# Layer 1's one-head attention and gate written between the chunks of layer 0's last two shared blocks, and layer 3's gate computed with its columns held in TensorE

## The chip, the core and the metric

The kernel runs on one core of a Trainium2 chip. The time is the device time of one execution in microseconds (us), the median of several runs; beside it stands one profiled execution with its span, from the first instruction to the last. The engines named are TensorE (PE, with its weight loads PEld), VectorE (DVE), ScalarE (ACT), GpSimd (POOL) and SyncE (SP), which issues most of the DMAs. Each engine works through its own instructions in the order in which they stand in its queue.

## The reference

A stack of four layers works on x, 2 sequences of 1,024 tokens of 256 values. Each layer adds a gated cross-attention to 77 context keys and then a gated feed-forward part, each on a normalised copy of x:

```python
x = x + tanh(g_xattn[l]) * xattn_l(layernorm(x), ctx, ctx, ...)
x = x + tanh(g_ffn[l])   * ffn_l(layernorm(x), ...)
```

Layers 0, 2 and 3 have 16 attention heads. Layer 1 has one head of width 256:

```python
Q = q @ Wq.T + bq;  K = k @ Wk.T + bk;  V = v @ Wv.T + bv
softmax(Q @ K.T / 16) @ V
```

The feed-forward parts are mixtures of experts, except layer 2's, which is quantised. Layer 0 has 8 experts, of which each token takes two, and a shared expert that every token takes; each is `swiglu((x@w1+b1)*(x@w3+b3))@w2+b2`. Layer 1 sends each token to the best of 16 experts; an expert takes at most 128 tokens, in the order of the tokens, so the places can be counted only when every token has its choice:

```python
gate = softmax(x @ Wg);  idx = argmax(gate)
loc = sum((cumsum(one_hot(idx)) - 1) * one_hot(idx))
```

Layer 3 takes `sigmoid(x @ gate_w)` over 8 experts in 4 groups, keeps two groups and two experts in them, and adds a shared expert too.

## The kernel before

**Tiles.** x lies on chip as 16 tiles `xs[i]` of 128 tokens by 256 values. Four of them make a block j of 512 tokens (`NB` = 4). A normalisation of a block (`layernorm`, L283-307) takes each tile's mean and variance on DVE (L290, L291), adds the small constant (L293), raises it to the power -1/2 on POOL (L295), makes four normalised tiles `h` on DVE (L299), turns them with eight transposes on TensorE into two PSUM banks `hTp` (L305), and copies these out, one on DVE (L306) and one on ACT (L307), as `hT`: channels on partitions, tokens along the row.

**Buffers.** PSUM has four banks for single results (`mm`) and two pairs of banks (`mm2`). The `h` tiles have four buffers in all, and the tiles `ga` into which expert outputs are gathered use the same four. Large weights (2 MB) have three buffers `wbig`; the attention's weights have one, `aw`.

**Order.** The code is written in an order of work, and a scheduler places its instructions in the engines' queues after that, with the waits that the data and the buffers need. Steps that are to overlap are therefore written between one another by hand: attention and expert jobs are generators that yield after each chunk.

**Layer 0's feed-forward part** (`ffn0`, L837-1052). After the gate, jobs run one after another (L1022-1041): shared blocks 0 and 1, 24 routed tiles of sorted tokens, shared blocks 2 and 3. A job's first half is `hidden` (L908-937): four chunks, each of two steps for a shared block; a step is four matmuls of 512 columns into one PSUM pair (L920), an eviction on ACT (L925) and one on DVE (L926). Its second half, `rest`, multiplies by the second weight (16 matmuls, L986) and adds to x (L990); it is written after the first chunk of the next job. When the last job is written, 32 gathers follow: for each tile two indirect DMAs from POOL (L1047), each added to x on DVE (L1051). Only then is a tile of x complete.

**Layer 1's attention** (`whole_attention`, L636-715) comes next: keys (L360) and values (L375) from the context once, then for each block the norm, the queries (L384 on TensorE, L663 on ACT), the scores (L671), the largest of them and the difference on DVE (L677, L679), the exponential on ACT (L680), the sums on DVE (L682-684), the probabilities turned on TensorE and copied on ACT (L690, L692), and the output (L700), weighted and added to x on DVE (L701). A loop staggers these steps over the blocks:

```python
for j in range(-2, NB + 1):
    has(turned, j)
    has(norm, j + 2)
    has(outputs, j)
    has(queries, j + 2)
    has(after, j - 1)
    has(scores, j + 1) if j >= 0 else None
```

`after` is `gate1` (L1060-1081): the norm for layer 1's experts, whose `h` tiles SP also stores to HBM, 32 small matmuls for the block's logits (`gate_logits`, L347), and the choice of the best expert on DVE, with an exponential on ACT. When all four blocks have their choice, `ffn1` counts the places: its first matmul is `cnt` (L1101). The experts' weights, 2 MB each, come by SP into the three `wbig` buffers.

**Layer 3's gate.** `turned(j)` (L1436) turns the normalised tiles of a block and copies them out (L1443, L1444). `gate` then computes the logits with `gate_logits`: for each of 16 tiles two matmuls with the turned tokens held in TensorE and 8 gate columns streamed. One sigmoid on ACT (L1453) reads the bank, and the choice of groups and experts on DVE follows, then the sorting, then the gathers of the routed tiles. The shared blocks' matmuls (`gus`, L1504) fill TensorE in the meantime.

Of the kernel before, what the change touches and what calls it, by code (L numbers as in the profile page):

```python
# [8 lines left out]
F32 = mybir.dt.float32  # L9
BF16 = mybir.dt.bfloat16  # L10
I32 = mybir.dt.int32
# [39 lines left out]
def flamingo_kernel(  # L51
# [18 lines left out]
    def mm(name, dt=F32, cols=512):  # L70
        return psA.tile([P, cols], dt, tag="mm", name=name)
# [237 lines left out]
    def new_hT(j, tagp):  # L309
        return hpool.tile([P, 2, TB], F32, tag=f"hT{j}", name=f"hT_{tagp}_{j}")  # L310
# [56 lines left out]
    def column(name, ec):  # L367
        c = COL[name]
        return cols[:, c, ec : ec + 1]
# [263 lines left out]
                behind(NB - 1)  # L633
        yield

    def whole_attention(l, after):  # L636

        w = attn_w.pop(l)
        scale = 1.0 / 16.0
        with ExitStack() as st:  # L640
            ap1 = st.enter_context(tc.tile_pool(name=f"at1_{l}", bufs=1))
            ap3 = st.enter_context(tc.tile_pool(name=f"at3_{l}", bufs=3))
            kT = ap1.tile([P, 2, 2 * NK], F32, tag="kT", name=f"kT{l}")
            pk = keys(l, "k", w, "k")
            for ec in range(2):
                V.tensor_scalar(kT[:, ec, :], pk[ec][:, 0 : 2 * NK], column(f"k{l}", ec), None, ALU.add)
            vs = []
            for b in range(2):
                vb = ap1.tile([NK, D], F32, tag=f"v{b}", name=f"vs{l}_{b}")
                pv = value(l, w, b)  # L650
                V.tensor_tensor(vb, pv[:NK, 0:D], w["bv"][:NK], ALU.add)
                vs.append(vb)
            hTs, qTs, prs, dens = {}, {}, {}, {}

            def norm(j):
                hTs[j] = new_hT(j, f"a{l}")
                layernorm(j, f"a{l}", hTs[j])

            def queries(j):
                qTs[j] = ap3.tile([P, 2, TB], F32, tag="qT", name=f"qT{l}_{j}")  # L660
                for ec in range(2):
                    pq = project(w, "q", hTs[j], ec, f"q{l}_{j}_{ec}")
                    S.activation(qTs[j][:, ec, :], pq, AF.Identity, bias=column(f"q{l}", ec))  # L663

            def scores(j):

                b = j // 2
                ps = mm(f"sc{l}_{j}")
                for k in range(4):
                    for ec in range(2):  # L670
                        T.matmul(  # L671
                            ps[:, k * NK : (k + 1) * NK], lhsT=qTs[j][:, ec, k * P : (k + 1) * P],
                            rhs=kT[:, ec, b * NK : (b + 1) * NK], start=(ec == 0), stop=(ec == 1),
                        )
                sc = ps[:, 0 : 4 * NK].rearrange("p (k n) -> p k n", n=NK)
                mx = ap3.tile([P, 4], F32, tag="mx", name=f"mx{l}_{j}")
                V.tensor_reduce(mx, sc, AX.X, ALU.max)  # L677
                pr = ap3.tile([P, 4, NK], F32, tag="pr", name=f"pr{l}_{j}")
                V.tensor_tensor(pr, sc, bcl(mx, NK), ALU.subtract)  # L679
                S.activation(pr, pr, AF.Exp, scale=scale)  # L680
                den = ap3.tile([P, 4], F32, tag="den", name=f"den{l}_{j}")
                V.tensor_reduce(den, pr, AX.X, ALU.add)  # L682
                V.reciprocal(den, den)
                V.tensor_scalar(den, den, tg[:, l : l + 1], None, ALU.mult)
                prs[j], dens[j] = pr, den

            def turned(j):
                pp = mm(f"pp{l}_{j}")
                for k in range(4):
                    T.transpose(pp[:NK, k * P : (k + 1) * P], prs[j][:, k, :], ident)  # L690
                prs[j] = ap3.tile([NK, TB], F32, tag="pT", name=f"pT{l}_{j}")
                S.copy(prs[j], pp[:NK, :])  # L692

            def outputs(j):
                for k in range(4):
                    i = 4 * j + k
                    if k % 2 == 0:
                        po = mm(f"o{l}_{i}")
                    half = po[:, (k % 2) * D : (k % 2 + 1) * D]
                    T.matmul(half, lhsT=prs[j][:, k * P : (k + 1) * P], rhs=vs[j // 2], start=True, stop=True)  # L700
                    V.scalar_tensor_tensor(xs[i], half, dens[j][:, k : k + 1], xs[i], ALU.mult, ALU.add)  # L701

            def has(step, j):
                if 0 <= j < NB:
                    step(j)

            for j in range(-2, NB + 1):
                has(turned, j)
                has(norm, j + 2)
                has(outputs, j)  # L710
                has(queries, j + 2)
                has(after, j - 1)
                has(scores, j + 1) if j >= 0 else None
                if j == -1:
                    scores(0)


    def route(nm, pool, pool2, oh, nf, nh, per, low, high):
# [107 lines left out]
        return sorted(range(nf + nh), key=lambda t: ((t + 0.5) / nf, 0) if t < nf else ((t - nf + 0.5) / nh, 1))  # L826


    wsh = {}

    def shared_first(n):
# [2 lines left out]
            out=wsh[n], in_=wbig0[8 * P * 4096 : 9 * P * 4096].rearrange("(r f) -> r f", f=4096)  # L834
        )

    def ffn0():  # L837
        h_dram = dram.tile([NT, D], F32, tag="h0_dram", name="h0_dram")
        eo_dram = dram.tile([NQ0 * P, D], F32, tag="eo0_dram", name="eo0_dram")
        with ExitStack() as st:  # L840
# [178 lines left out]
            wrow2 = f1.tile([P, nt], I32, tag="wrow2", name="wrow2")  # L1019
            V.tensor_scalar(wrow2, wrow, rest0, None, ALU.add)  # L1020

            jobs = [(shared, 0), (shared, 1)] + [(routed, t) for t in order] + [(shared, 2), (shared, 3)]  # L1022
            left = None
            for n, (job, arg) in enumerate(jobs):
                if n == 0:
                    load(order[0])
                    load(order[1])
                steps, rest = job(arg)
                for ic, _ in enumerate(steps):
                    if ic == 0 and left is not None:  # L1030
                        left()
                    if ic == 1 and n + 1 < len(jobs) and jobs[n + 1][0] is routed:
                        turn(jobs[n + 1][1])
                left = rest
                if job is routed:
                    at = order.index(arg) + 2
                    if at < nt:
                        load(order[at])
                    elif at == nt:
                        shared_first(1)  # L1040
                        shared_rest(1)
            left()
            prefetch(1)
            for i in range(NTI):
                for k in range(2):
                    ga = lnp.tile([P, D], F32, tag="h", name=f"ga0_{i}_{k}", bufs=4)
                    G.indirect_dma_start(  # L1047
                        out=ga, out_offset=None, in_=eo_dram,
                        in_offset=bass.IndirectOffsetOnAxis(ap=row[:, k * NTI + i : k * NTI + i + 1], axis=0),
                    )  # L1050
                    V.scalar_tensor_tensor(xs[i], ga, wk[:, k, i : i + 1], xs[i], ALU.mult, ALU.add)  # L1051


    NE, C, NF = 16, 128, 8
    h1_dram = dram.tile([NT, D], F32, tag="h_dram", name="h_dram")
    eo1_dram = dram.tile([NE * C, D], F32, tag="eo_dram", name="eo_dram")
    oh1 = gs1.tile([P, NTI, NE], BF16, tag="oh1", name="oh1")
    place1 = gs1.tile([P, NTI, 2, NE], BF16, tag="place1", name="place1")
    wgt1 = gs1.tile([P, NTI], F32, tag="wgt1", name="wgt1")
    row1 = gs1.tile([P, NTI], I32, tag="row1", name="row1")  # L1060

    def gate1(j):
        def keep(i, h):
            nc.sync.dma_start(out=h1_dram[i * P : (i + 1) * P, :], in_=h)

        hT = new_hT(j, "f1")
        layernorm(j, "f1", hT, each=keep)
        pl = gate_logits(j, hT, 8, NE, "f1")
        lg = gp.tile([P, NB, NE], F32, tag="g1l", name=f"g1l_{j}")
        V.tensor_copy(lg, pl)  # L1070
        blk = slice(4 * j, 4 * j + 4)
        first_max(lg, NE, oh1[:, blk, :], f"f1_{j}")

        V.tensor_scalar(place1[:, blk, 0, :], oh1[:, blk, :], iota_p, None, ALU.mult)
        V.tensor_tensor(place1[:, blk, 1, :], oh1[:, blk, :], bcl(tile128[:, blk], NE), ALU.mult)
        m = gp.tile([P, NB], F32, tag="g1m", name=f"g1m_{j}")
        V.tensor_reduce(m, lg, AX.X, ALU.max)
        V.tensor_tensor(lg, lg, bcl(m, NE), ALU.subtract)
        S.activation(lg, lg, AF.Exp)
        V.tensor_reduce(m, lg, AX.X, ALU.add)  # L1080
        V.reciprocal(wgt1[:, blk], m)

    def combine1(j):
        for i in range(4 * j, 4 * j + 4):
# [338 lines left out]
    def ffn3():  # L1423
# [4 lines left out]
        with ExitStack() as st:  # L1428
# [6 lines left out]
            def turned(j):  # L1435
# [7 lines left out]
                V.tensor_copy(hT[:, 0, :], pts[0])  # L1443
                S.copy(hT[:, 1, :], pts[1])  # L1444
                hTs[j] = hT

            def gate():

                pl = mm("lg_f3")
                for j in range(NB):  # L1450
                    gate_logits(j, hTs[j], 24, 8, "f3", pl[:, 32 * j : 32 * j + 32])
                sf = f1.tile([P, NTI, 8], F32, tag="g3s", name="g3s")
                S.activation(sf, pl[:, 0 : NTI * 8].rearrange("p (k n) -> p k n", n=8), AF.Sigmoid)  # L1453
                V.tensor_tensor(sf, sf, bcm(bc[:, 8:16], NTI), ALU.add)
                gs = f1.tile([P, NTI, 4], F32, tag="g3g", name="g3g")
                V.tensor_tensor(gs, sf[:, :, 0::2], sf[:, :, 1::2], ALU.add)
# [119 lines left out]

                return rest

            for j in range(NB):
                turned(j)  # L1580
            picked = gate()
# [49 lines left out]

    whole(heads_attention(0, ahead=lambda j: tables() if j == 2 else shared_first(0) if j == 3 else None))
    attn_w[1] = load_attn(1)
    ffn0()
    q2["pool"] = tc.alloc_tile_pool(name="w2p", bufs=1, side="right")
    whole_attention(1, gate1)
    attn_w[2] = load_attn(2)
    attn2 = heads_attention(2, combine1, norm2)
    next(attn2)
# [143 lines left out]
```

## Time and profile before

| | |
|---|---|
| time, median of 3 runs | 1594.83 us (1592.28 to 1599.27) |
| profiled execution: own time | 1592.78 us |
| its span | 1591.0 us |
| mean granted TensorE clock | 0.918 |
| instructions | 18,196 |
| TensorE busy in the 71.8 us from 654.4 (layer 0's last blocks) | 65.12 us, clock 0.98 |
| TensorE busy in the 88.9 us from 726.2 (layer 1's attention and gate) | 66.64 us, clock 0.72 |
| TensorE busy in the 52.5 us from 1383.0 (layer 3's gate and routing) | 43.56 us, clock 0.83 |

All times are of one profiled execution, in us from the start of the span. A row of the chain or of the waits begins with the start and the length of an instruction or group, then its engine, its line in the code and what it wrote and read; a bracket gives the time that the engine had stood idle before it and what ended that. A row of stage windows gives the window, its length, and the busy time of each engine with the number of instructions; the last three numbers are the granted clock (1 is full), the busy share of the DMA engines and what they moved in GB/s. Busy time is not the same as time on the path: what sets the end of a stage is read from the chain.

### The profile page before, as it was taken

The numbers are of one execution on the slowest core, as the hardware profiler recorded it, in microseconds if no ns is written. First come the engines' busy times: TensorE is split into PE (matmuls) and PEld (weight loads), VectorE is DVE, ScalarE is ACT, GpSimd is POOL, SyncE is SP. The second block draws the span as 40 slices with busy tenths as digits, with TensorE's granted clock in tenths as the row PEclk, the third lists the DMA queues.
The fourth block names the chain that finished last, engine by engine and source line by source line (L and its number), as shares of the span: only waits on it lengthen the run. The fifth ranks groups of instructions, "written<-read, shape, count | busy, mean of one in ns | idle before, by whom it ended". The sixth has DMA issues, their size and how long they took to land.

```text
span 1591.0 us, 18196 instructions
## 1 busy us (share of the span) xinstructions
PE 1370.0 (86%) x6844; PEld 914.4 (57%) x6844; DVE 888.3 (56%) x2167; ACT 399.5 (25%) x671; POOL 316.8 (20%) x367
## 2 busy tenths in 40 slices
PE   6999996999999999988759996899965999985773
PEld 3453444888888888445658883345334544544562
DVE  7676676444444444566543117667789666682124
ACT  1332430233333333212101111122354233201230
POOL 3200002212212120341021104300014300005651
PEclk9999997999999999999759997989987999987887
DMA  4001005555646555312216772000000000023535
GB/s 159 4 14 49 27 1 208 177 209 183 229 173 227 203 176 215 103 50 73 76 39 241 294 284 63 28 2 1 1 27 20 1 14 14 27 80 102 172 127 175
DMA packets 48363, 169.87 MB, mean 107 GB/s; under 512 B 9040, under 2 KB 27635, under 8 KB 42259
## 3 DMA queue, kind: packets, MB, share of 16 engines
q0 software_dynamic: 15600, 88.23, 15.9%
q1 hardware_dynamic: 25664, 74.33, 13.4%
q10 hardware_dynamic: 7010, 6.15, 1.3%
q8 instruction: 54, 0.88, 0.2%
q14 instruction: 35, 0.28, 0.1%
HBM read 147.97 MB, written 20.71 MB: 106 GB/s over the span
## 4 chain that ended last, share of the span: by engine, by line
PE 66%; DVE 16%; DMA 8%; issue 5%; POOL 2%; ACT 2%; another core or an unknown queue 1%; ACTq 0%; POOLq 0%; DVEq 0%; SPq 0%
PE hr L920 17%; PE hs L920 6%; PE sc L498 5%; PE eo L1004 4%; DMA wbig<-in_wbig_dram 4%; PE q L384 3%; PE as L574 3%; PE sT L546 3%; PE gur L1504 2%; PE h L1158 2%; PE av L574 2%; PE sT L553 2%; PE lg_f L347 2%; PE o L589 2%; PE eo_s L986 1%
## 5 line engine op out<-in xcount | busy, mean ns | idle before, releaser
L920 PE MATMUL hr<-xgT0s,w 128*128 128x256 f32 (+1 forms) x1536 | 299.9, 346 | 9.4 <-DVE ulr L926 9.2
L920 PEld LDWEIGHTS hr<-xgT0s,w 128*128 128x128 f32 x1536 | 246.3, 191 | 52.7 <-DVE ulr L926 22.1
L561 ACT ACTIVATE pT<-sT 78x1024 f32<-78x1024 f32 x96 | 92.7, 1015 | 231.8 <-PE sT L553 209.0
L498 PE MATMUL sc<-kbd,qT 128*128 128x308 f32 x384 | 126.6, 442 | 6.9 <-DVE qT L480 6.2
L920 PE MATMUL hs<-hT_f,w0s 128*128 128x512 f32 x256 | 119.4, 611 | 6.7 <-DVE x L1051 2.6
L508 DVE TENSOR_REDUCE nm<-sc 128x4 f32<-128x308 f32 x192 | 88.6, 474 | 46.3 <-PE sc L504 33.5
L926 DVE SCALAR_TENSOR_TENSOR ulr<-hr,w,ulr 128x256 f32<-128x256 f32 (+1 forms) x96 | 41.6, 433 | 127.0 <-ACT ulr L925 126.6
L579 DVE RECIPROCAL rz<-as 128x512 f32<-128x512 f32 x24 | 80.5, 3356 | 29.6 <-PE as L574 29.6
L498 PEld LDWEIGHTS sc<-kbd,qT 128*128 128x128 f32 x384 | 68.5, 197 | 44.4 <-issue 20.1
L920 PEld LDWEIGHTS hs<-hT_f,w0s 128*128 128x128 f32 x256 | 47.6, 195 | 59.8 <-issue 46.7
L925 ACT ACTIVATE ulr<-hr,w 128x256 f32<-128x256 f32 (+1 forms) x96 | 41.7, 434 | 143.6 <-PE hr L920 142.9
L1004 PE MATMUL eo<-w,hid_r 128*128 128x256 f32 x312 | 77.5, 379 | 0.0
L384 PE MATMUL q<-hT_a,aw 128*128 128x512 f32 x128 | 69.7, 678 | 6.5 <-DVE hT_a L306 4.5
L1158 PE MATMUL h<-xgTs,wbig 128*128 128x128 f32 x512 | 61.8, 281 | 6.6 <-DMA wbig<-in_wbig_dram 6.5
L948 POOL DMA_INDIRECT w<-in_wbig_dram,r_wr_f x24 | 24.2, 1008 | 212.9 <-PE hr L920 130.8
L1158 PEld LDWEIGHTS h<-xgTs,wbig 128*128 128x128 f32 x512 | 60.5, 196 | 9.9 <-issue 8.3
L1496 DVE TENSOR_TENSOR sg_r<-gur,sg_r 128x256 f32<-128x256 f32 (+1 forms) x24 | 9.0, 375 | 97.4 <-ACT sg_r L1495 64.0
L1004 PEld LDWEIGHTS eo<-w,hid_r 128*128 128x128 f32 x312 | 57.8, 190 | 7.6 <-issue 0.5
L1504 PE MATMUL gur<-xT3s,w 128*128 128x256 f32 (+1 forms) x192 | 50.6, 418 | 12.5 <-ACT xT3s L1552 9.1
L925 ACT ACTIVATE ugr<-hr,w 128x256 f32<-128x256 f32 (+1 forms) x96 | 41.7, 434 | 77.7 <-PE hr L920 70.9
L1171 PE MATMUL eo<-wbig,hh 128*128 128x256 f32 x256 | 59.9, 379 | 0.0
L926 DVE SCALAR_TENSOR_TENSOR ugr<-hr,w,ugr 128x256 f32<-128x256 f32 (+1 forms) x96 | 41.5, 432 | 31.4 <-ACT ugr L925 18.0
(451 smaller groups left out, 2305.9 us busy)
## 6 DMA issues: line engine op xcount, KB each, us to landing
wbig<-in_wbig_dram SPq DMA_DIRECT2D x17, 2048.0 KB
w<-in_wbig_dram SPq DMA_DIRECT2D x24, 384.0 KB
w0s<-in_wbig_dram SPq DMA_DIRECT2D x2, 2048.0 KB
h_dram<-h_f SPq DMA_DIRECT2D x32, 128.0 KB
y<-y_dram SPq DMA_DIRECT2D x4, 1024.0 KB
eo_dram<-eo0s SPq DMA_DIRECT2D x15, 256.0 KB
x<-in_x_dram SPq DMA_DIRECT2D x4, 512.0 KB
aw<-in_aw_dram SPq DMA_DIRECT2D x2, 1024.0 KB
```

The costliest lines, as they stand in the source:

```text
L384: T.matmul(pq, lhsT=w[m][:, dc, ec * P : (ec + 1) * P], rhs=hT[:, dc, :], start=(dc == 0), stop=(dc == 1),)
L498: T.matmul(ps[:, 0 : 4 * NK], lhsT=qTs[j][:, ec, k * P : (k + 1) * P], rhs=kbd[b][:, ec, 4 * hf : 4 * hf + 4, :].rearrange("p h k -> p (h ...
L508: V.tensor_reduce(nms[j][:, k, 2 * hf : 2 * hf + 2, ec, :], ps[:, 0 : 4 * NK].rearrange("p (r i k) -> p r i k", i=2, k=NK), AX.X, ALU.max, ...
L561: S.activation(pT[:, 2 * a : 2 * a + 2, :], pp[a][:NK1], AF.Exp, scale=scale)
L574: T.matmul(po[32 * r : 32 * r + 32, :], lhsT=lhsT(r, i)[:nk], rhs=pTs[j, ec, i][:nk, r, :], start=(i == 0), stop=(i == 1),)
L579: V.reciprocal(rz, pz)
L920: T.matmul(both[a][:, wi, :], lhsT=w13[:, dc, wi, a, ic * P : (ic + 1) * P], rhs=rhs(dc), start=(dc == 0), stop=(dc == 1),)
L925: S.activation(uu, both[a][:, 0, :], AF.Identity, bias=bias[:, 0, a, ic : ic + 1])
L926: V.scalar_tensor_tensor(uu, both[a][:, 1, :], bias[:, 1, a, ic : ic + 1], uu, ALU.add, ALU.mult)
L1004: T.matmul(po[:, s * D : (s + 1) * D], lhsT=hid[:, ic, s * P : (s + 1) * P], rhs=w2[:, ic, :], start=(ic == 0), stop=(ic == 3),)
L1158: T.matmul(ph[:, fc // 4, (fc % 4) * C : (fc % 4 + 1) * C], lhsT=w1[:, dc, fc * P : (fc + 1) * P], rhs=xgTs[e][:, dc, :], start=(dc == 0), ...
L1504: T.matmul(pa[:, s, 0:n], lhsT=w[:, s, dc, :], rhs=rhs(dc), start=(dc == 0), stop=(dc == 1))
```

## The change

**Layer 1 moves into layer 0.** `whole_attention` no longer runs its own loop. It makes the keys and values and gives back its five steps, which `ffn0` calls between the chunks of shared blocks 2 and 3. The gathers move as well: those of blocks 0 and 1 stand after the first chunk of shared block 2, with the keys and values, those of blocks 2 and 3 after its second and third chunk. `gate1` is split into `gate1_norm` (the norm with the stores) and `gate1` (logits and choice). What is left of attention and gate when shared block 3 is done is written behind it in a fixed order. The attention's pools lie on the other side of the on-chip memory, open from before `ffn0` to its end, with two buffers instead of three for `pr` and `pT`. The instructions of these steps themselves stay as they were.

**Layer 3's gate.** The 32 gate columns are now the held operand (8 of them are layer 3's, columns 24 to 31) and the turned tokens are streamed, 512 at a time: two matmuls for each block, written in `turned(j)` right behind its copies, into 32 partitions of one bank that is taken ahead of the first block. The result has tokens along the row, so two half copies (DVE and ACT) take it out, four transposes turn it back, and the sigmoid reads columns 24 to 31 of each group of 32.

```diff
-    def whole_attention(l, after):
+    def whole_attention(l, st):
...
+        return norm, queries, scores, turned, outputs
...
+    def gate1_norm(j):
+        def keep(i, h):
+            nc.sync.dma_start(out=h1_dram[i * P : (i + 1) * P, :], in_=h)
+
+        hT1[j] = new_hT(j, "f1")
+        layernorm(j, "f1", hT1[j], each=keep)
+
+    def gate1(j):
+        pl = gate_logits(j, hT1[j], 8, NE, "f1")
...
-            jobs = [(shared, 0), (shared, 1)] + [(routed, t) for t in order] + [(shared, 2), (shared, 3)]
+            jobs = [(shared, 0), (shared, 1)] + [(routed, t) for t in order]
...
+            s2, rest2 = shared(2)
+            next(s2)
             left()
             prefetch(1)
...
+            gathered(0)
+            gathered(1)
+            norm, queries, scores, turned1, outputs = whole_attention(1, st1)
+            next(s2)
+            gathered(2)
+            next(s2)
+            norm(0)
+            gathered(3)
+            next(s2)
+            queries(0)
+            norm(1)
+            s3, rest3 = shared(3)
+            next(s3)
+            rest2()
+            scores(0)
+            queries(1)
+            next(s3)
+            turned1(0)
+            scores(1)
+            norm(2)
+            next(s3)
+            outputs(0)
+            queries(2)
+            turned1(1)
+            next(s3)
+            gate1_norm(0)
+            scores(2)
+            outputs(1)
+            rest3()
+        gate1(0)
+        norm(3)
+        turned1(2)
+        gate1_norm(1)
+        queries(3)
+        outputs(2)
+        gate1(1)
+        scores(3)
+        gate1_norm(2)
+        turned1(3)
+        gate1(2)
+        outputs(3)
+        gate1_norm(3)
+        gate1(3)
...
+                for dc in range(2):
+                    T.matmul(
+                        pl[32 * j : 32 * j + 32, :], lhsT=gw[:, dc, :], rhs=hT[:, dc, :],
+                        start=(dc == 0), stop=(dc == 1),
+                    )
...
-                pl = mm("lg_f3")
-                for j in range(NB):
-                    gate_logits(j, hTs[j], 24, 8, "f3", pl[:, 32 * j : 32 * j + 32])
+                lgs = f3.tile([P, TB], F32, tag="sg", name="lgs3", bufs=4)
+                V.tensor_copy(lgs[:, 0:256], pl[:, 0:256])
+                S.copy(lgs[:, 256:512], pl[:, 256:512])
+                pt = mm("lgT_f3")
+                for k in range(4):
+                    T.transpose(pt[:, k * P : (k + 1) * P], lgs[:, k * P : (k + 1) * P], ident)
                 sf = f1.tile([P, NTI, 8], F32, tag="g3s", name="g3s")
-                S.activation(sf, pl[:, 0 : NTI * 8].rearrange("p (k n) -> p k n", n=8), AF.Sigmoid)
+                S.activation(
+                    sf.rearrange("p (j k) n -> p j k n", k=4),
+                    pt.rearrange("p (k j n) -> p j k n", k=4, j=4)[:, :, :, 24:32], AF.Sigmoid,
+                )
...
+            pl = mm("lg_f3")
             for j in range(NB):
                 turned(j)
...
-    ffn0()
+    with ExitStack() as st1:
+        ffn0(st1)
     q2["pool"] = tc.alloc_tile_pool(name="w2p", bufs=1, side="right")
-    whole_attention(1, gate1)
```

The queues that the moved steps pass: POOL has the 32 gathers, the powers of the norms and the memsets of layer 2's attention; SP has the stores of layer 1's `h` tiles, the expert weights and layer 2's attention weights.

## The prediction

> **What bounds the kernel now.** I read the page first: engines' shares, then the chain that ended last.
>
> ```profile
> PE 1370.0 (86%) x6844; PEld 914.4 (57%) x6844; DVE 888.3 (56%) x2167; ACT 399.5 (25%) x671; POOL 316.8 (20%) x367
> ...
> PE 66%; DVE 16%; DMA 8%; issue 5%; POOL 2%; ACT 2%; another core or an unknown queue 1%; ACTq 0%; POOLq 0%; DVEq 0%; SPq 0%
> ```
>
> TensorE carries two thirds of the chain, but that is a mean over stages. So I cut out the two stretches that the change merges: from the second chunk of shared block 2 to the end of shared block 3 (654.4 to 726.2), and one-head attention with layer 1's gate, up to the routing's first matmul, `cnt` (726.2 to 815.1). Columns: length, busy time of PE, its weight loads, DVE, ACT, POOL, then granted clock, DMA share, GB/s.
>
> ```profile
> 654.40:726.20 71.80, 65.12 (x179) 33.74 (x178) 46.41 (x106) 14.43 (x22) 32.01 (x33) 0.98 0.27 84
> 726.20:815.10 88.90, 66.64 (x288) 49.81 (x286) 49.01 (x176) 16.66 (x29) 9.32 (x12) 0.72 0.17 52
> 772.00:828.00 56.00, 33.58 (x143) 27.92 (x142) 29.14 (x111) 4.80 (x11) 7.94 (x11) 0.51 0.13 42
> ```
>
> The second stretch is bound by latency: no engine is full, and TensorE runs at 0.51 of its clock from 772 on. The chain within both, in order of time (start, length, what):
>
> ```profile
> 680.08 4.72 PE hs L920 x8
> ...
> 698.66 20.60 PE hs L920 x48
> 719.26 3.47 PE eo_s L986 x16
> ...
> 735.04 5.47 PE q L384 x8
> ...
> 742.32 3.67 PE q L384 x8
> ...
> 782.48 3.60 PE lg_f L347 x16
> ...
> 809.90 3.61 PE lg_f L347 x16
> ...
> 815.11 0.40 PE cnt L1101
> ```
>
> 48 records of `hs` in 20.6 us: a step (four matmuls, one PSUM pair) takes 3.43 us when fed. `q` takes 5.47 us after idleness and 3.67 us warm. Gathers are timed by POOL, and their adds sit between evictions in DVE's queue:
>
> ```profile
> 658.12 0.95 POOL L1047 DMA_INDIRECT ga<-eo_dram,r_row_f  x1 [52.99 <-DMA eo_dram<-eo0s]
> ...
> 660.83 0.48 DVE L1051 SCALAR_TENSOR_TENSOR x<-ga,wk,x 128x256 f32<-128x256 f32 x1 [0.86 <-DMA ga<-eo_dram,r_row_f]
> ...
> 680.08 3.70 PE L920 MATMUL hs<-hT_f,w0s 128*128 128x512 f32 x8 [1.62 <-DVE x L1051]
> ```
>
> TensorE idled there because the eviction that frees its PSUM pair stood behind a gather's add. Layer 3's gate, by the same chain:
>
> ```profile
> 1383.24 6.36 PE lg_f L347 x48
> 1389.60 1.91 PE gus L1504 x2
> 1391.51 3.21 PE lg_f L347 x16
> 1394.72 15.23 PE gus L1504 x32
> ```
>
> 64 small records take 9.6 us, at half clock by the end; DVE waits 11 us for them, then works 34.85 of 37 us (1398 to 1435) until the expert gathers start.
>
> **The change, part 1: up to the end of shared block 3.** The built kernel's order shows attention's work between the chunks as written. I walk it from 654.4 with rows of this trace. Keys and values now come first: `k` 1.21, `v` 1.89, together 2.95, so the next step starts at 657.4. Six steps remain, 20.6 us if fed. DVE's order puts 3 gather adds ahead of this chunk's first eviction, 7 ahead of the second, 15 ahead of the fourth. 20 gathers were issued from 658.12 to 682.36, 1.276 each, with the add 2.7 later: the 16th add can run at 658.12 + 15 x 1.276 + 2.7 = 680.0. With the eviction (0.75) the last step runs 680.9 to 684.3, 6.3 late.
>
> Block 0's norm waits for its power on POOL, queued behind the 24th gather: 658.12 + 23 x 1.276 + 1.25 = 688.7, power 1.05, h at 689.9. Behind it stand on TensorE the transposes, q and all of shared block 3: idle 684.3 to 690.4. q starts at 693.0. Taken cold, 5.47, it ends at 698.4, two steps of block 3 at 705.4. The last eight gathers take slots that h's transposes free at 691.0 (they share four); last issue 699.9, add 702.6, stats and an eviction, power, h: transposes 707.4 to 708.8. From there TensorE is fed, warm: block 2's output 7.07, sc 1.91, q 3.67, two steps 6.86, pp 0.66, sc 1.91, hTp 1.04, two steps 6.86, o 2.1, q 3.67, pp 0.66, two steps 6.86, hTp 1.04, sc 1.91, o 2.1, block 3's output 7.07: 55.4. With 1 us for short waits, E = 765.2. The merged work is 98 us of matmuls plus 8 us of the two idle stretches and 1.8 cold, where 72 us stood.
>
> **Part 2: from E to `cnt`.** Block 3 of x is complete only at E; its norm, query, scores, softmax, output, norm and gate remain, with other blocks' steps in the queues ahead. DVE: block 0's logits (1.93) and their copy stand ahead of the last stats: variance E+4.0, h E+5.4 (power with its waits 1.4). Transposes and copies, half clock, 3.0 (as 806.89 to 809.84): E+8.4. q would start here, but TensorE has block 1's gate transposes ahead of it, whose stats, power and h take until E+11.9. q with six transposes inside, 6.4: E+18.3. Outputs of block 2 and block 1's logits, warm, 4.0; sc 1.9: E+24.2. Softmax with a gate's small operations 2.2, then block 2's stats (ahead of block 3's transposed probabilities) 2.0, power, h: E+29.7. Transposes and pp: E+32.9. Block 2's logits, cold, 3.6; outputs to their last add 4.9 (793.56 to 798.50): E+41.4. Stats 1.4; from the variance to `cnt` 9.6 as 805.56 to 815.11: E+52.4 = 817.6, against 815.1: **+2.5**. So 89 us become 52, and 72 become 111.
>
> **The clock, where a rule and the rows differ.** Rows: after the last dense matmuls end at 766.6, the clock is 1.00 to 772 and 0.50 from 776, and stays there to 828 though TensorE is busy 33.6 of those 56 us. "TensorE: Matmul & The Clock Gate" (Part 1: The HAM clock gate) of the Trainium skill has half clock as the default, released by a window of about 3.4 us of activity and lost after an idle one; its Part 4 adds that transposes do not count as busy. It speaks against this change, which makes idle windows at 684 and at E+2. If q releases the clock and only long idleness takes it, everything after q is warm, 8 us less: 809.6. If it stays half as in the rows, q, o, logits and sc cost 7.3 more: 824.9. I take release by q (row 735.04: 5.47, then 3.67) and loss 6 us later (766.6 to about 772.8). Both ends go into the range.
>
> **Part 3: edits hidden.** Four more ACT table loads (1.28 each, row L680) fall between evictions on an engine busy 20%; exposed, they cost 5. POOL's four memsets for attention 2 (2.1 us) now precede block 3's power, done by E+2.3 where the variance comes at E+4.0; late, they add their lateness. SP: block 0's four stores stand ahead of the third expert weight, 2 MB in some 9 us, issued near 752 instead of 719 but used after 855. Layer 2's weights wait on SP for block 3's q (E+18 instead of 766.7), used at 855.8, with block 2's stores behind them, due E+30. 70 us of cover each: nothing. If it were gone, the expert gathers would wait for those stores one for one.
>
> **Part 4: layer 3's gate.** 64 records at 9.6 become 16 of 512 columns at 0.434, 6.9, three quarters of them between the transposes. In the built order the last pair ends about 1391.5; two half copies 0.5, a table load now behind ACT's copy (1.28), four transposes beside it: sigmoid at 1393.8, against 1394.8. The shared matmuls then run warm (0.87 a matmul, the rows between had up to 1.03), and DVE's first wait for them (1.74) shrinks: 1.7 more. **-2.7**; bounds +1 (one PSUM bank held over all transposes delays them) and -6 (all idleness of DVE there).
>
> **Sum.** +2.5 - 2.7 = -0.2 on the profiled execution: span 1591.0, its own time 1592.78. The median of the runs is 1594.83, 2.05 above, with runs from 1592.28 to 1599.27. Forecast 1594.
>
> **Rivals.** *Faster: latency is truly hidden.* Clock warm after q (-8), and evictions not held by gathers (up to -8, E = 757): 1594 - 8 = 1586, with both 1578. For it: both merged stretches had idle TensorE, 29 us in all. Against: block 3's chain still starts at E, and 16 us of it is other blocks' work queued in between. *Slower: the gathers' slots.* Gathers share four buffers with h, so each waits for an add that now waits behind evictions. There is 1.9 us of slack (add of k ends 3.2 after its issue, slot needed at 5.1). If adds slip past it and the pace goes from 1.28 to 1.7, E moves by 32 x 0.42 = 13: 1607. It decides above 1.53, where 32 x 0.25 = 8. For it: before, the 21st gather waited 6.25 us for such an add. *Only moved:* layer 3's gain lost in DVE's queue: 1597; it lies within the likeliest.
>
> **Chances.** 0.5% is 8 us, about what a measurement of this kernel can tell. Likeliest (no difference, own range 1586 to 1602) 0.47; faster 0.33; slower 0.20. Range 1577 to 1608, the outer part of each rival left out.
>
> **What would show it.** Right: shared block 3's output ending near 765, `cnt` near 817, TensorE idle before block 0's transposes for some 6 us, half clock in the last 25 us before `cnt`, gate 3's sigmoid a microsecond after 1393 less the shift. Wrong: `cnt` under 808 with the clock at 1.0 (faster), or gathers slower than 1.5 us each (slower).

## The result and the profile after

The changed kernel takes 1589.02 us (1587.43 to 1592.55), the kernel before 1594.12 us (1590.45 to 1599.67); the ratio is 0.9965, 95% interval 0.995 to 0.998: by the ratio 5.6 us faster. The profiled execution took 1588.63 us, its span is 1586.9 us, 4.1 below that of before.

The page of the changed kernel has these lines in the places of the first two shown of before:

```profile
PE 1358.2 (86%) x6798; PEld 901.4 (57%) x6800; DVE 890.0 (56%) x2168; ACT 403.7 (25%) x676; POOL 318.0 (20%) x367
...
PE 31%; DVE 11%; DMA 7%; issue 3%; POOL 2%; ACT 1%; another core or an unknown queue 1%; POOLq 0%; DVEq 0%; ACTq 0%; SPq 0%
```

TensorE is busy 12 us less, with 46 records fewer. Layer 3's gate accounts for 44 of them: its logits take 16 records in place of 64, and four transposes came in. The shares of the chain can't be set beside those of before: here they add up to 56%, so the chain was followed back through part of the span only. The stage windows can (columns as before), cut where TensorE's state changes between the keys and `cnt`:

```profile
657.40:684.30 26.90, 21.40 (x51) 8.97 (x50) 16.38 (x36) 3.79 (x6) 19.37 (x20) 1.00 0.37 108
684.30:712.00 27.70, 16.86 (x37) 7.44 (x35) 17.02 (x45) 5.75 (x9) 13.71 (x15) 0.75 0.22 63
712.00:767.30 55.30, 55.30 (x227) 37.33 (x226) 35.80 (x90) 19.27 (x26) 2.02 (x2) 0.97 0.13 48
767.30:817.80 50.50, 32.30 (x146) 26.07 (x145) 26.34 (x110) 6.27 (x13) 5.96 (x8) 0.63 0.19 65
```

The third row is what interleaving does well: 55.3 us without a gap. The second is the hole in front of it, the fourth the chain of block 3 with its 18 us of idleness. Both are read from the timeline and the chain of the same kernel. First the hole, with the variances that VectorE makes for the two norms (start, length, engine, line; the bracket is the idle time before):

```profile
688.43 0.94 POOL L1068 DMA_INDIRECT ga<-eo_dram,r_row_f  x1 [0.30 <-DVE mv_a L291]
689.62 0.17 DVE L293 TENSOR_SCALAR ve_a<-mv_a 128x4 f32<-128x4 f32 x1 [0.41 <-DVE x L1072]
691.83 1.04 POOL L295 TENSOR_TENSOR rs_a<-ve_a,nhalf 128x4 f32<-128x4 f32 x1 [2.46 <-DVE x L1072]
...
704.70 1.01 POOL L1068 DMA_INDIRECT ga<-eo_dram,r_row_f  x1 [0.30 <-issue]
709.88 0.16 DVE L293 TENSOR_SCALAR ve_a<-mv_a 128x4 f32<-128x4 f32 x1
710.20 1.04 POOL L295 TENSOR_TENSOR rs_a<-ve_a,nhalf 128x4 f32<-128x4 f32 x1 [4.48 <-DVE ve_a L293]
```

The first power stands behind the 24th gather (688.43) in GpSimd's queue, the second behind the 32nd (704.70). But GpSimd was through with these gathers at 689.4 and 705.7, and neither power started then. The variances came later, at 689.8 and 710.0: in VectorE's queue they stand behind 22 and all 32 of the gathers' adds. So the second power waited 4.5 us for VectorE and started as soon as its variance was there. The first waited 0.4 us for its variance and another 2.0 us that these rows do not explain. TensorE idles for both norms, and each bracket names the `h` that the power makes possible:

```profile
693.38 1.97 PE L305 MATMUL hTp_a<-ident,h_a 128*128 128x128 f32 x8 [7.86 <-DVE h_a L299]
695.92 6.65 PE L384 MATMUL q<-hT_a,aw 128*128 128x512 f32 x8 [0.57 <-DVE hT_a L306]
...
711.84 1.76 PE L305 MATMUL hTp_a<-ident,h_a 128*128 128x128 f32 x8 [2.41 <-DVE h_a L299]
```

Then the chain from the end of shared block 3's output to the routing (start, length, what):

```profile
762.13 5.18 PE eo_s L1007 x24
767.31 1.71 PE lg_f L347 x16
...
782.12 3.47 PE q L384 x6
...
789.02 1.85 PE sc L670 x16
...
798.90 3.31 PE lg_f L347 x16
802.22 3.71 PE o L699 x8
...
812.55 3.61 PE lg_f L347 x16
816.19 0.24 DVE g1l L836
...
817.76 0.37 PE cnt L1142
```

`cnt` starts at 817.76, where before it started at 815.11 (this execution was 1.0 us later when it reached layer 1's part): the interleaving brought nothing there. Layer 3's gate did. Of before, VectorE's waits from the sigmoid to the first gathers of layer 3's routed tiles (total, times, longest):

```profile
DVE g3s L1454 <- ACT g3s L1453: 11.1, 1, 11.1
DVE sg_s L1496 <- ACT sg_s L1495: 2.7, 2, 1.7
```

and of the changed kernel:

```profile
DVE g3s L1507 <- ACT g3s L1503: 2.0, 1, 2.0
DVE sg_s L1549 <- ACT sg_s L1548: 0.6, 1, 0.6
```

Its 32 records of shared matmuls behind the gate take 13.73 us in the chain, against 15.23 before:

```profile
1393.92 0.44 PE lgT_f L1501 x4
1394.36 13.73 PE gus L1557 x32
```

So VectorE waits 0.6 us for their first evictions in place of 2.7. The granted clock went with it: before, it was 0.67 from 1383.2 to 1394.7, while the small records ran, and 0.91 over the shared matmuls behind them; in the changed kernel it is 1.00 from 1381.0 to 1408.1. The 11.1 us became 2.0 because it copies half the logits itself right ahead of the sigmoid; that shift alone is worth nothing.

### The profile page after: what moved, and what is told of

The parts are those of the page before. It is cut to its first block, busy times and chain, and to the rows that moved or that the text cites. A ratio compares the mean times of both kernels' runs of the same rounds, so it can differ in the third digit from the quotient of the medians.

```text
span 1586.9 us, 18081 instructions
## 1 busy us (share of the span) xinstructions
PE 1358.2 (86%) x6798; PEld 901.4 (57%) x6800; DVE 890.0 (56%) x2168; ACT 403.7 (25%) x676; POOL 318.0 (20%) x367
## 4 chain that ended last, share of the span: by engine, by line
PE 31%; DVE 11%; DMA 7%; issue 3%; POOL 2%; ACT 1%; another core or an unknown queue 1%; POOLq 0%; DVEq 0%; ACTq 0%; SPq 0%
DMA wbig<-in_wbig_dram 4%; PE sc L498 4%; PE q L384 2%; PE h L1199 2%; PE as L574 2%; PE gur L1557 2%; PE sT L546 2%; PE sT L553 2%; PE eo L1212 1%; PE av L574 1%; PE hs L941 1%; PE o L589 1%; PE gus L1557 1%; DVE hmax L1390 1%; PE eo_s L1007 1%
## 5 line engine op out<-in xcount | busy, mean ns | idle before, releaser
L1199 PE MATMUL h<-xgTs,wbig 128*128 128x128 f32 x512 | 62.7, 283 | 5.7 <-DMA wbig<-in_wbig_dram 5.7
L947 DVE SCALAR_TENSOR_TENSOR ugr<-hr,w,ugr 128x256 f32<-128x256 f32 (+1 forms) x96 | 41.5, 433 | 31.4 <-ACT ugr L946 15.4
```

The lines of the kernel that those rows point to most:

```text
L947: V.scalar_tensor_tensor(uu, both[a][:, 1, :], bias[:, 1, a, ic : ic + 1], uu, ALU.add, ALU.mult)
L1199: T.matmul(ph[:, fc // 4, (fc % 4) * C : (fc % 4 + 1) * C], lhsT=w1[:, dc, fc * P : (fc + 1) * P], rhs=xgTs[e][:, dc, :], start=(dc == 0), ...
```

## The experiments

The span was cut into stretches that can be compared from one execution to the next: **A**, from the last gather of inputs of layer 0's routed tiles to `cnt` (layer 1's part); **B**, from there to the last reciprocal of layer 3's attention (untouched); **C**, from there to the first gather of inputs of layer 3's routed tiles (the gate's part); **D**, from there to the first addition of the outputs (untouched). Each row is one profiled execution, in us, with the ratio to the kernel before that was timed beside it. The stretches are differences of times given to 0.1 us.

| kernel | A | B | C | D | ratio, 95% interval |
|---|---|---|---|---|---|
| before | 220.7 | 555.6 | 64.8 | 136.2 | 1 |
| before, once more | 224.6 | 552.1 | 67.2 | 137.1 | 1.0001 (0.9988 to 1.0014) |
| changed | 222.4 | 553.8 | 62.0 | 134.0 | 0.9965 (0.995 to 0.998) |
| changed, once more | 222.6 | 553.8 | 62.0 | 135.1 | 0.9965 (0.9953 to 0.9977) |
| gate alone | 220.7 | 551.8 | 62.1 | 134.9 | 0.9966 (0.9949 to 0.9983) |
| layer 1 alone | 223.1 | 550.5 | 67.1 | 135.2 | 0.9998 (0.998 to 1.0015) |
| norms early, shared buffers | 220.6 | 554.4 | 63.1 | 140.7 | 0.9999 (0.998 to 1.0018) |
| own buffers only | 220.7 | 553.9 | 62.1 | 139.0 | 0.9976 (0.9963 to 0.999) |
| norms early, own buffers | 212.8 | 550.5 | 63.2 | 132.8 | 0.9899 (0.9878 to 0.992) |
| other order at the end | 215.8 | 550.7 | 63.3 | 134.1 | 0.992 (0.9896 to 0.9943) |
| both orders | 206.9 | 553.5 | 62.1 | 135.9 | 0.9877 (0.9847 to 0.9906) |
| clock kept | 217.0 | 555.0 | 63.2 | 132.3 | 0.9974 (0.9958 to 0.9991) |
| clock kept, once more | 218.9 | 551.3 | 63.2 | 137.3 | 0.9946 (0.9928 to 0.9963) |
| both orders, clock kept | 198.3 | 554.5 | 63.3 | 134.5 | 0.9811 (0.9787 to 0.9835) |

B and D hold the same instructions in all and still differ by 5 and 8 us. That is the scale below which two spans say nothing; A and C are read by themselves.

**Gate alone.** Of the diff only the part in layer 3:

```diff
+                for dc in range(2):
+                    T.matmul(
+                        pl[32 * j : 32 * j + 32, :], lhsT=gw[:, dc, :], rhs=hT[:, dc, :],
+                        start=(dc == 0), stop=(dc == 1),
+                    )
...
-                pl = mm("lg_f3")
-                for j in range(NB):
-                    gate_logits(j, hTs[j], 24, 8, "f3", pl[:, 32 * j : 32 * j + 32])
...
```

> The kernel before with layer 3's gate changed as in the diff, layer 1 as before. Theory A (the prediction's sum: gate -2.7, layer 1's part +2.5): 1594.1 - 2.7 = 1591.4, the first gathers of layer 3's routed tiles 2.7 us earlier against the attention ahead of them. If the 2 us that the changed kernel gained behind those gathers are the gate's too: 1589.3. Theory B (the gain is layer 1's interleaving): 1594, no difference.

1587.35 us against 1593.43; by the ratio 5.4 us faster, 2.7 to 8.1. Theory B is out. Theory A's 2.7 us lies at the near end of the interval, and C is 62.1 us where 64.8 stood. The edit changes the form of the logits and their place between the transposes together; which of the two brings the gain is not shown.

**Layer 1 alone.** The other half: the changed kernel with layer 3's gate put back.

```diff
-                for dc in range(2):
-                    T.matmul(
-                        pl[32 * j : 32 * j + 32, :], lhsT=gw[:, dc, :], rhs=hT[:, dc, :],
-                        start=(dc == 0), stop=(dc == 1),
-                    )
...
```

> The changed kernel with layer 3's gate put back as before. Theory A: cnt at about 817.7 as in the changed kernel, 2.5 us later than before, and the whole time 1594 to 1597. Theory B: 1589, as the changed kernel, although cnt is late; then the gain must lie between cnt and layer 3.

1593.94 against 1593.43, ratio 0.9998: no difference that can be measured. The two parts add up (5.4 + 0.3 = 5.7 of 5.6 us). So the gain of the whole change is layer 3's gate, and the large rewrite is neutral within 3 us.

**Why the rewrite is neutral: the hole.** The norms of blocks 0 and 1 move next to the gathers that they need.

```diff
+            norm, queries, scores, turned1, outputs = whole_attention(1, st1)
             gathered(0)
+            norm(0)
             gathered(1)
-            norm, queries, scores, turned1, outputs = whole_attention(1, st1)
             next(s2)
+            next(s2)
+            norm(1)
             gathered(2)
+            queries(0)
             next(s2)
-            norm(0)
             gathered(3)
-            next(s2)
-            queries(0)
-            norm(1)
...
-                        ga = lnp.tile([P, D], F32, tag="h", name=f"ga0_{i}_{k}", bufs=4)
+                        ga = f3.tile([P, D], F32, tag="ga0", name=f"ga0_{i}_{k}", bufs=4)
```

(The room for the buffers comes from `qT`, two instead of three.)

> The changed kernel with the norms of blocks 0 and 1 written right after the gathers that they need (so their powers stand on GpSimd behind some 12 and 22 gathers instead of 24 and 32), query 0 ahead of the last chunk of shared block 2, and with four buffers of their own for the gathers. Theory: the two idle stretches of TensorE (7.9 and 2.4 us, before the transposes of blocks 0 and 1) are the power's place in GpSimd's queue; they go, about 4 us of a new wait come in the third chunk, the end of shared block 3's output moves from 767.3 to about 757, and cnt with it: 1589.0 - 10 = 1579. Rival: VectorE's queue (gather adds between evictions) is what holds TensorE; then the waits only move and the time stays within 3 us of 1589.

1578.06 us, ratio 0.9899: 10.5 us faster than the changed kernel by the ratios. The timeline of this kernel shows the first power behind the 13th gather, the block's transposes after 3.5 us of idleness in place of 7.9, no gap ahead of block 1's, and the end of the last shared output at 759.0 in place of 767.3:

```profile
676.26 1.05 POOL L295 TENSOR_TENSOR rs_a<-ve_a,nhalf 128x4 f32<-128x4 f32 x1
...
677.87 1.54 PE L305 MATMUL hTp_a<-ident,h_a 128*128 128x128 f32 x8 [3.54 <-issue]
...
694.55 1.42 PE L305 MATMUL hTp_a<-ident,h_a 128*128 128x128 f32 x8
...
753.62 5.34 PE L1007 MATMUL eo_s<-w02s,hid_s 128*128 128x256 f32 x24
```

The theory said 1579. So the hole was the place of the two norms behind gathers that their blocks do not need. That it was GpSimd's queue alone, as the theory has it, is not shown: the edit moves a norm's statistics and variance forward in VectorE's queue together with its power in GpSimd's, and in the changed kernel the variances came last. Here it is GpSimd that comes last: the first variance is there at 674.3, and the power waits 2.0 us more for the 13th gather to end.

**The same without buffers of their own.** As above, but `ga` stays with tag `h`, and `qT` has its three buffers again.

> The same new places of the norms of blocks 0 and 1, but the gathers keep sharing four buffers with h. If the power's place in GpSimd's queue alone is the cause of the idle stretches, as with own buffers: 1578. If the shared buffers matter once the norms stand between the gathers (the h tiles hold all four until TensorE has turned them, so no gather can be issued for 3 to 5 us, twice): 1582 to 1588.

Ratio 0.9999, A 220.6 against 212.8 with own buffers. The gathers do wait, and longer than the expected 3 to 5 us: none is issued from 667.4 to 674.0 and from 685.3 to 694.3. The brackets of this kernel's timeline put 4.4 and 6.1 us of that down to the powers' waits for their variances; then come the powers themselves, and 1.2 and 1.8 us until slots are free. TensorE is idle again, now after shared block 2's output:

```profile
671.76 1.04 POOL L295 TENSOR_TENSOR rs_a<-ve_a,nhalf 128x4 f32<-128x4 f32 x1 [4.36 <-DVE ve_a L293]
691.38 1.04 POOL L295 TENSOR_TENSOR rs_a<-ve_a,nhalf 128x4 f32<-128x4 f32 x1 [6.05 <-DVE ve_a L293]
...
717.39 3.67 PE L670 MATMUL sc<-kT,qT 128*128 128x77 f32 x16 [6.60 <-issue]
```

The expected time (1582 to 1588, a ratio up to 0.996) was missed on the high side; 6 us of its span lie in D, which the edit does not touch, so how much of the total is the edit's stays open. A alone says that the new order needs the buffers.

**The buffers without the new order.**

```diff
-                        ga = lnp.tile([P, D], F32, tag="h", name=f"ga0_{i}_{k}", bufs=4)
+                        ga = f3.tile([P, D], F32, tag="ga0", name=f"ga0_{i}_{k}", bufs=4)
```

> The changed kernel's order, only with four buffers of their own for the gathers. The gathers of block 3 no longer wait for the transposes of block 0 (1.9 and 1.3 us in the changed kernel); block 1's power stands behind the last of them, so it comes some 3 us earlier: 1586. If the power's place is what counts and not the buffers: within 3.5 us of 1589.

Ratio 0.9976, inside the changed kernel's interval; A is 1.7 us shorter. Buffers alone are worth little or nothing, so the prediction's rival of the gathers' slots was no danger here. In this trace GpSimd is through with all gathers at 700.3, but the second norm's variance comes at 706.6, and TensorE still idles 2.0 us for it: freeing GpSimd does not help a norm that VectorE holds back.

**The chain behind block 3.**

```diff
         gate1(0)
         norm(3)
         turned1(2)
-        gate1_norm(1)
         queries(3)
         outputs(2)
-        gate1(1)
+        gate1_norm(1)
         scores(3)
-        gate1_norm(2)
+        gate1(1)
         turned1(3)
-        gate1(2)
         outputs(3)
+        gate1_norm(2)
         gate1_norm(3)
+        gate1(2)
         gate1(3)
```

> The changed kernel with another order behind shared block 3: block 3's query ahead of block 1's gate norm, and block 3's turned probabilities and output ahead of block 2's gate norm. Theory (in the 50.5 us from the end of shared block 3's output to cnt, other blocks' work stands ahead of block 3's chain): query 3 starts at about 776 instead of 780 to 782, its output ends near 796 instead of 806, cnt at 811 to 813: 1583 to 1585. Rival (the tail is limited by the sum of the engines' work at half clock, so the work moved behind block 3's output costs as much there): cnt within 2 us of 817.8 and 1588 to 1590.

1581.61 us, ratio 0.992: 7.2 us faster than the changed kernel, A 6.6 shorter, `cnt` at 812.9. Its timeline, in an execution that reached this part 1.7 us later:

```profile
768.81 1.85 PE L347 MATMUL lg_f<-gw,hT_f 128*128 128x16 f32 x16
...
777.14 4.63 PE L384 MATMUL q<-hT_a,aw 128*128 128x512 f32 x8
...
791.05 3.88 PE L699 MATMUL o<-vs,pT 77*128 77x256 f32 x8 [0.67 <-ACT pT L691]
...
812.90 0.40 PE L1142 MATMUL cnt<-oh,earlier 128*128 128x256 bf16 x1 [2.39 <-DVE oh L329]
```

The output of block 3 starts 22.2 us after block 0's logits, where the changed kernel needs 34.9 (802.22 less 767.31). Half of that gain is given back behind it, where two norms and two gates now stand together.

**Both orders.** The two edits together.

> The changed kernel with both edits at once: norms of blocks 0 and 1 right behind their gathers with buffers of their own for the gathers (alone: 11 us faster than the changed kernel, cnt 9.6 earlier) and the new order behind shared block 3 (alone: 7.4 us faster, cnt 6.6 earlier, counted from the last gather of layer 0's routed tiles). The two lie on either side of the end of shared block 3's output. If they are two separate stretches of one chain the gains add: 1589.0 - 11 - 7.4 = 1570.6, cnt near 803. If an engine's sum of work became the bound: 1575 or more.

1573.22 us, ratio 0.9877, beside a kernel before that took 1590.63. Against 1594.12, on which the expectation rests, the ratio makes 1574.5: the time lies between the two theories and does not decide. The sum of the two gains would be 0.9854, which lies in the interval, and A is 206.9, 15.5 below the changed kernel (9.6 + 6.6 expected). By A, the two stretches lie one behind the other on one chain.

**The clock at the end.** Products that nobody reads, in TensorE's idle stretches:

```diff
+    def warm(n):
+        pw = mm(f"warm_{len(fillers)}")
+        fillers.append(pw)
+        for _ in range(n):
+            T.matmul(pw[:, 0 : 4 * NK], lhsT=ident, rhs=ctxT.rearrange("p c n -> p (c n)"), start=True, stop=True)
...
+        warm(10)
         norm(3)
         turned1(2)
+        warm(9)
         gate1_norm(1)
...
+        warm(14)
         gate1_norm(2)
...
+        warm(11)
         gate1_norm(3)
```

> The changed kernel with 10, 9, 14 and 11 matmuls of 308 columns, whose result nobody reads, in the four idle stretches of TensorE behind shared block 3 (0.26 us each at full clock). The prediction put 8 us on the clock there: half from 6 us after the last dense work to the query, full from the query for some 6 us, half to cnt. If that is so and the added matmuls keep the clock at 1.0: cnt some 6 us earlier, at 812, 1583. Rival: the clock is not what the path waits for (norms wait for VectorE and GpSimd), or the added matmuls stand in the way: 1588 to 1592.

In the changed kernel the clock came back with the query and was lost again, as the prediction had it; windows of 4 us, the granted clock is the third number from the end:

```profile
776.00:780.00 4.00, 1.52 (x4) 1.03 (x5) 2.08 (x9) 0.01 (x1) 1.01 (x1) 0.50 0.18 59
780.00:784.00 4.00, 4.00 (x10) 2.23 (x10) 0.69 (x1) 0.72 (x2) 0.00 (x0) 0.53 0.22 74
784.00:788.00 4.00, 4.00 (x22) 3.01 (x21) 1.25 (x3) 1.24 (x2) 0.00 (x0) 1.00 0.34 83
...
792.00:796.00 4.00, 0.00 (x0) 0.00 (x0) 2.78 (x17) 0.46 (x1) 1.01 (x1) 0.75 0.00 0
796.00:800.00 4.00, 3.92 (x19) 3.79 (x19) 1.69 (x5) 1.17 (x2) 0.00 (x0) 0.50 0.39 131
800.00:804.00 4.00, 4.00 (x16) 3.38 (x15) 1.41 (x8) 0.00 (x0) 0.00 (x0) 0.50 0.00 0
```

With the added matmuls it is 1.00 from 767 to 812, and the last two blocks' logits take 1.96 us each in place of 3.52 and 3.60. A matmul turned out to be two records of 0.27 us, so the additions were twice as long as meant and held up what stood behind them (block 3's transposes by 1.5 us); A fell by 5.4 us all the same. Its timed ratio, 0.9974, did not show that, so it was run once more beside the changed kernel.

> The changed kernel with the added matmuls once more, beside the changed kernel on the same chip. In its trace cnt came 5.4 us earlier, but its timed ratio to before (0.9974) was no better than the changed kernel's (0.9965, on another chip). If the 5.4 us reach the end: 5 us faster than the changed kernel of this call. If they are lost behind cnt (the experts' weights, a lower clock later): the same time within 2 us.

> The changed kernel once more, beside the kernel before, for a second trace of each on one chip. From the last gather of layer 0's routed tiles to cnt: 222.4 us within 0.5 if that stretch is the same in every execution; from the last reciprocal of layer 3's attention to the gathers of its routed tiles 62.0; from there to the first addition of the outputs 134 if the gate sets it, anything from 132 to 141 if it is the execution's own.

> The kernel before once more. The same stretches: 220.7, 64.8 to 67.1, and the last one 136.2 if the 2 us there are the gate's, anything from 132 to 141 and not tied to the gate if they are the execution's own.

On this chip: 1588.15 with the clock kept, 1589.96 changed, ratios 0.9946 and 0.9965, 3.0 us apart with intervals that meet (0.9928 to 0.9963, 0.9953 to 0.9977). A is 218.9 against 222.6. The gain of 3.7 to 5.4 us in A is there; that it reaches the end in full is not shown by these two.

The repeated traces settle three things. A of the changed kernel is steady (222.4, 222.6). A with the old order is not: 220.7 in the kernel before and with the gate alone, then 224.6 in the kernel before once more. Of these 3.9 us, 1.5 had come by shared block 2's output, 1.1 in the first query (6.55 us in place of 5.47) and 1.4 in steps behind it. D is 137.1 with the old gate and 135.1 with the new on this chip, but 132.3 to 140.7 over all with the new one: the spread of D is the executions' own and can't be put down to the gate.

**Both orders with the clock kept**, with 6, 2, 5 and 4 added matmuls ahead of `norm(3)`, `turned1(3)`, `gate1_norm(2)` and `gate1_norm(3)`:

> The version with both orders changed, with 6, 2, 5 and 4 added matmuls (0.52 us each) in TensorE's idle stretches behind shared block 3. If the clock is on the path there as in the changed kernel: another 4 to 5 us, from the last gather to cnt 202 instead of 206.9. If its tail waits for VectorE and GpSimd: no gain, 206 to 208.

1564.22 us, ratio 0.9811: 30 us faster than before, 24.5 faster than the change as made. A is 198.3, 8.6 below the version without the additions, more than the 4 to 5 us expected; why more is not shown. The timeline has the additions and, behind them, gaps under 1 us where 2 to 3.5 us were:

```profile
761.83 3.36 PE L1143 MATMUL warm<-ctxT,ident 128*128 128x308 f32 x12
765.49 0.76 PE L305 MATMUL hTp_a<-ident,h_a 128*128 128x128 f32 x4 [0.30 <-DVE h_a L299]
...
785.07 1.32 PE L305 MATMUL hTp_f<-ident,h_f 128*128 128x128 f32 x8 [0.27 <-DVE h_f L299]
786.23 2.24 PE L1143 MATMUL warm<-ctxT,ident 128*128 128x308 f32 x8
789.32 1.53 PE L305 MATMUL hTp_f<-ident,h_f 128*128 128x128 f32 x8 [0.85 <-DVE h_f L299]
```

## Why the prediction was right, and where it was off

**The case.** It put no measurable difference as the likeliest. The ratio is 0.9965, a gain of 0.35%, inside its 0.5%, and 1589.0 lies in the range; the sum of -0.2 us came out as -5.6. That is a gain clear of the noise (0.995 to 0.998), which the sum did not foresee: its two terms nearly cancelled, the first was too large a loss and the second too small a gain.

**Part 1, up to the end of shared block 3.** Predicted 765.2, measured 767.3. The course is as predicted: idleness of 6.1 us ahead of block 0's transposes (7.9), a cold query, a second wait at block 1's norm, then a full TensorE. For the first norm the prediction had GpSimd's queue as the last wait. The 24th gather was through at 689.4, close to its 688.7, but the variance came 0.4 us after that and the power another 2.0 us later. For the second norm it had the right path, through the last gather's add and the statistics on VectorE. Four sizes were off and partly cancelled: the gathers began 1.0 us later in this execution; the power came 2.46 us after GpSimd was free, which the sum did not have; the cold query took 6.65 us, not 5.47; and the full part took 53.7 us, not 56.4.

**Part 2, to `cnt`.** Predicted 52.4 us, measured 50.5. The steps are those of the sum, counted from E, the end of shared block 3's output: block 3's query ends at E+18.3 (forecast 18.3), its scores at E+23.6 (24.2), and block 2's transposes start at E+28.8 (29.7). That `cnt` came at 817.8, where 817.6 was forecast, is luck: 2.1 us too little in part 1 and 1.9 too much here cancel. And "+2.5" rests on one execution of the kernel before. Means of A are 222.0 over three executions of the old stretch (220.7, 220.7, 224.6) and 222.7 over three of the new (222.4, 222.6, 223.1), and the timed difference is -0.3 us (-3.2 to +2.4). "+2.5" is the term that was mis-sized: these put it at nothing to +1.

**The clock.** The prediction set a page of the Trainium skill ("TensorE: Matmul & The Clock Gate", Part 1: The HAM clock gate) against the rows, and took release by the query and loss 6 us after the next stop. The release is as taken: 0.53 until 784, then 1.00. The loss came sooner: 0.75 from 792 to 796 is full clock for half of that window, so it fell near 794, some 3 us after the scores had ended at 790.9. The page's window of about 3.4 us of activity fits the query, which started near 779. It does not fit what follows: TensorE was busy from 796.1 to 805.9 with transposes, logits and block 3's output, and the clock stayed at 0.50. What sets that work apart from the query's is not shown. The same section calls the window free-running, so that the release comes at another point in each execution; that agrees with the kernel before, whose first query took 5.47 us in one execution and 6.55 in another. The clock's record in the changed kernel's trace agrees too: it changes at 770.14, 783.80, 794.04 and 835.00, which are 4, 3 and 12 times 3.41 us apart. "8 us less, if everything is warm" was tested: A fell by 5.4 and 3.7 with additions that were too long.

**Part 3.** The edits costed at nothing stayed hidden as far as these runs show: the power of block 3's norm starts 0.1 us after its variance (770.99, 770.85), so the memsets ahead of it did not hold it, and B does not differ between the orders beyond its own spread.

**Part 4, layer 3's gate.** Predicted -2.7. C is 66.4 us over three executions with the old gate and 62.7 over eleven with the new: -3.7. In the prediction's two parts: the sigmoid comes 0.8 us earlier (23.5 us after the last reciprocal, against 24.3 over three; predicted 1.0), and from it to the gathers 39.2 against 42.1, 2.9 us (predicted 1.7). The second is the mis-sized term: the profile shown had 2.7 us of VectorE's waits for the shared matmuls, the two other executions with the old gate 4.0 and 4.3, and those with the new gate 0.6 where they were read. The timed gain of the gate alone, 5.4 us (2.7 to 8.1), takes in 3.7; whether there is a remainder is not shown.

**The rivals.** *Latency truly hidden* did not happen in the change as made, but time was to be had in both places that it named. The hole gave 9.6 us in A, though by moving the norms and not, as the rival had it, by freeing evictions from the gathers. The clock gave 5.4 and 3.7 us by itself, and 8.6 on top of both orders. The new order of block 3's chain, where the prediction saw 16 us of other blocks' work, gave 6.6. *The gathers' slots*: 1.26 us from one gather to the next, far from 1.53. Over all 32, with the first norm and its wait for slots in between, it is 1.47, where the sum had 1.35. The slots became a loss only when the norms were moved between the gathers without buffers of their own.

## What to carry to other kernels

Steps written between dense chunks are hidden only if nothing that they need stands in another engine's in-order queue behind work that is not theirs: here two norms stood behind up to sixteen gathers that their blocks did not need, with their variances in VectorE's queue and their powers in GpSimd's, and TensorE idled 10 us for them. Before a queue is blamed, the rows must show which of the two came last. Merging two stages hides the first blocks and leaves the last block's chain bare; what decides is then the order in that chain, where the last block's own steps must come first. A stretch that repeats in a trace is measured by several executions before a term of 2 us is booked on it.

## What the runs showed of the hardware

Small added products in gaps of 3 to 5 us held the granted clock at 1.00 for 45 us, where its mean was 0.63 without them. TensorE's being busy was not enough by itself: through 9.8 us of transposes, logits of 16 columns and block 3's output the clock stayed at 0.50. The same 32 matmul records behind layer 3's gate took 15.4, 16.7 and 16.9 us after 64 records of 8 columns, at a clock of 0.91, 0.84 and 0.82, and 13.9 us after 16 of 512 columns, at 1.00. And stretches with the same instructions differ between executions by more than the change is worth: 5 us in B, 8 us in D.
